# Feed-forward rows turned by VectorE and DMA, two weight loads issued by ScalarE, input rows read a group sooner

## The chip, the cores and the metric

The kernel runs on one core of a Trainium2 chip. The metric is the device time of one execution in microseconds; the time before is the median of three runs. The profile is of one further execution.

## The reference

x has the shape (4, 512, 512): four batches of 512 tokens of 512 features, f32. Four blocks follow one another, each added to the residual x:

```
x = x + attention_a(layernorm(x))   # 16 heads of 128, 4 key/value heads: half causal softmax with rotary,
                                    # half a gated linear recurrence over the tokens; then Wo
x = x + ffn(layernorm(x))           # ternary weights w1, w2 (1408x512) and w3 (512x1408)
x = x + attention_b(layernorm(x))   # 16 heads; weights are FP4 codes times a scale for each 32 rows
x = x + ffn(layernorm(x))

def ffn(x):
    x1, x2 = x @ quantize(w1).T, x @ quantize(w2).T
    return (sigmoid(x1) * x2) @ quantize(w3).T
```

The layernorm has no gain or bias: (x - mean) / sqrt(var + 1e-5).

## The kernel before

x stays in SBUF in 16 tiles of 128 tokens by 512 features (x0 to x15), four tiles (chunks) to a batch. Every product contracts over features, so normalised rows must be turned round: features on partitions. In the feed-forwards and in the second attention an f32 operand is kept as a rounded half hi and a remainder lo, both float32r, and each product is made twice, with hi and with lo.

**First attention** (`first_attention_gentle`). The steps are chunks: 4 batches by 4 key/value groups by 4 chunks of 128 tokens, so a group is four steps. `step(n)` issues the pieces of several chunks interleaved: A is the query projection (mm<-wq,xnT), B its softmax, rotation and a transfer through DRAM (queries, qdT), C transposes, D scores and softmax, own the recurrence's scores in a chunk (sc<-qdT,kdT), F the weighted values, G the output projection (mm<-wo,oT) with the add to x. TensorE's order in these steps is written by hand (`manual_schedule`); the other engines are ordered by the scheduler, except where `in_place` keeps an instruction where the program has it. Each group needs its Wq and its Wo (1 MB each, 16 loads of each). `load` reads the next batch's four x tiles at the first step of the group before, and `layernorm_steps` is advanced piece by piece by `next(ln)`: statistics (bn_stats, bn_aggr, POOL's power, three Newton steps), then for each chunk xn on VectorE, four transposes on TensorE into a tp bank, and a copy. All loads named here are on SyncE's queue. Beside this runs `quantise`, which makes the feed-forward's ternary weights and writes them to DRAM (`blocks`). `ahead(50, 0)` makes the first feed-forward's rows of batch 0 in the last steps, and the transposes for batch 1 follow where the scheduler puts them.

**Feed-forward** (`feed_forward`). The weights are loaded once for each feed-forward, in 22 loads (line 262). For each batch b: for each of 11 f, 16 products (sc<-xnhi,block and sc<-xnlo,block), sigmoid on ScalarE, hT on VectorE, hi on ScalarE, hlo on VectorE; then for each of 4 chunks c a product y of 22 matmuls (mm), the add to x and, in the second feed-forward, the store of the output. While batch b is computed, `halved` makes the rows of batch b + 1 by `layernorm_steps`: xn, four transposes (line 165), a split from PSUM into xnhi and xnlo (lines 120 and 121). All 512 tokens of a batch are the moving operand of its first products, so these need all four chunks. A caller's `next(steps)` per f from f = 2 on (two at f = 2) advances it.

During the first feed-forward the second attention prepares its weights (`prepare`): for each half weight a fetch (a load of the codes and four of the scales, SyncE, lines 284 and 287), two multiplications on POOL (line 292), two roundings on ScalarE (line 297), two comparisons on VectorE (line 303) and a write to DRAM (line 304). There are three such tiles.

xn has one buffer (`bufs=1`) in the pool `lnp`.

Of the kernel before, what the change touches and what calls it, by code (L numbers as in the profile page):

```python
# [9 lines left out]
F32 = mybir.dt.float32  # L10
# [9 lines left out]
P = 128  # L20
B, S, C = 4, 512, 512
NC = S // P
# [52 lines left out]
def hybrid_block(ctx: ExitStack, tc: tile.TileContext, a: dict, out: bass.AP):  # L75
# [42 lines left out]
    def split(hi, lo, src, engine=nc.vector):  # L118

        nc.scalar.copy(hi, src)  # L120
        engine.tensor_tensor(lo, src, hi, ALU.subtract)

    def layernorm_steps(b, sink, tag="tp", apart=False):

        mv = lnp.tile([P, NC, 2], F32, tag="mv", name="mv")
        rstd = lnp.tile([P, NC], F32, tag="rstd", name="rstd")

        def moments(c):  # L130
            st = lnp.tile([P, 6], F32, tag="st", name="st")
            nc.vector.bn_stats(st, xs[b * NC + c])  # L132
            nc.vector.bn_aggr(mv[:, c, :], st)

        def scales(at):

            var = lnp.tile([P, NC], F32, tag="var", name="var")[:, at]
            nc.vector.tensor_scalar(var, mv[:, at, 1], LN_EPS, None, ALU.add)
            r = rstd[:, at]
            nc.gpsimd.tensor_tensor(r, var, power[:, : r.shape[1]], ALU.pow)  # L140
            t = lnp.tile([P, NC], F32, tag="newton", name="newton")[:, at]
            nc.vector.tensor_tensor(t, r, r, ALU.mult)
            nc.vector.tensor_tensor(t, t, var, ALU.mult)
            nc.vector.tensor_scalar(t, t, -0.5, 1.5, ALU.mult, ALU.add)
            nc.vector.tensor_tensor(r, r, t, ALU.mult)

        if not apart:
            for c in range(NC):
                moments(c)
                if c == 1:  # L150
                    yield
            scales(slice(0, NC))
        for c in range(NC):
            if apart:
                moments(c)
                scales(slice(c, c + 1))
            else:
                yield
            xn = lnp.tile([P, C], F32, tag="xn", name="xn", bufs=1)
            nc.vector.tensor_scalar(xn, xs[b * NC + c], mv[:, c, 0:1], rstd[:, c : c + 1], ALU.subtract, ALU.mult)  # L160
            if not apart:
                yield
            tp = bank(tag, [P, NK, P])
            for k in range(NK):
                nc.tensor.transpose(tp[:, k, :], xn[:, k * P : (k + 1) * P], ident)  # L165
            sink(c, tp)
# [5 lines left out]
    def halved(pool, b):  # L172

        halves = [pool.tile([P, NK, S], F32R, tag=f"xn{n}", name=f"xn{n}") for n in ("hi", "lo")]
        return halves, layernorm_steps(b, lambda c, tp: split(*(h[:, :, c * P : (c + 1) * P] for h in halves), tp))

    def whole(pool, b):

# [31 lines left out]


    pieces = [[(k, f, n) for k in range(NK) for f, n in ((0, 6), (6, NF - 6))]] * 2 + [[(0, f, 1) for f in range(NF)]]
    part = per.tile([P, 3, NF], F32, tag="part", name="part")
    thr = per.tile([P, 3, 2], F32, tag="thr", name="thr")

    def quantise(pool, tag):


        def piece(n, k, f, m):
            w = pool.tile([P, 6 * P], F32, tag="w", name="w")[:, : m * P if n < 2 else C]  # L220
            if n < 2:
                in_place(nc.sync.dma_start(w, a[f"w{n + 1}T"][k * P : (k + 1) * P, f * P : (f + m) * P]))
            else:
                in_place(nc.sync.dma_start(w, a["w3T"][f * P : (f + 1) * P, :]))
            return w

        for n in range(3):
            for i, p in enumerate(pieces[n]):
                w = piece(n, *p)
                yield  # L230
                in_place(nc.scalar.activation(w, w, AF.Abs, accum_out=part[:, n, i : i + 1]))
                yield
            row = pool.tile([P, 1], F32, tag="row", name="row")
            nc.vector.tensor_reduce(row, part[:, n, : len(pieces[n])], AX.X, ALU.add)
            yield
            tot = bank(tag, [P, 1])
            nc.tensor.matmul(tot, lhsT=ones, rhs=row, start=True, stop=True)

            up, down = thr[:, n, 0:1], thr[:, n, 1:2]
            nc.vector.tensor_scalar(up, tot, 1.0 / (C * FF), QUANT_EPS, ALU.mult, ALU.add)  # L240
            nc.vector.tensor_scalar(down, up, -0.5, None, ALU.mult)
            nc.vector.tensor_scalar(up, up, 0.5, None, ALU.mult)
            yield
            for k, f, m in pieces[n]:
                w = piece(n, k, f, m)
                yield
                low = pool.tile([P, 6 * P], BF16, tag="low", name="low")[:, : w.shape[1]]
                in_place(nc.vector.tensor_scalar(low, w, down, None, ALU.is_lt))
                t = pool.tile([P, 6 * P], F32R, tag="tern", name="tern", bufs=1)[:, : w.shape[1]]
                in_place(nc.vector.scalar_tensor_tensor(t, w, up, low, ALU.is_gt, ALU.subtract))  # L250
                yield
                if n < 2:
                    in_place(nc.sync.dma_start(blocks[f : f + m, :, n, k * P : (k + 1) * P].rearrange("f p j -> p f j"), t.bitcast(F32).rearrange("p (f j) -> p f j", j=P)))
                else:
                    in_place(nc.sync.dma_start(blocks[f, :, n, :], t.bitcast(F32)))
# [53 lines left out]
    def first_attention_gentle(base, extra):  # L309
# [6 lines left out]
        with ExitStack() as st:  # L316
# [55 lines left out]
            class Group:  # L372
# [8 lines left out]

                def load_wq(self):
                    self.wq = one.tile([P, NK, HG * D], F32, tag="wq", name="wq")
                    nc.sync.dma_start(self.wq, a["Wq"][:, self.g * HG * D : (self.g + 1) * HG * D].rearrange("(k p) n -> p k n", p=P))

                def load_wo(self):
                    self.wo = late.tile([P, HG, C], F32, tag="wo", name="wo")
                    nc.sync.dma_start(self.wo, a["Wo"][self.g * HG * D : (self.g + 1) * HG * D, :].rearrange("(h p) n -> p h n", p=P))

                def project(self, c):  # L390
                    acc = bank("mm", [P, 2, D])
# [158 lines left out]
            def step(n):  # L550
                nonlocal ln
                m, p = divmod(n + 7, NC)
                at = lambda i: chunks.get(n + i) if n + i < last else None
                if (m + 1) % KV == 0 and (m + 1) // KV < B:
                    if p == 0:
                        load((m + 1) // KV)
                    if p == 1:
                        ln = normalise((m + 1) // KV)
                    if p > 1:
                        next(ln)  # L560
# [514 lines left out]
    def feed_forward(base, last, first):  # L1075

        with ExitStack() as st:
# [5 lines left out]
            ws = [block((soon, soon) if f < 2 else pools, f) for f in range(NF)]  # L1083
            xn = first
            for b in range(B):
                ready, steps = halved(base, b + 1) if b + 1 < B else (None, iter(()))
                hid = []
                for f, (w, _) in enumerate(ws):
                    xs12 = []
                    for n in range(2):  # L1090
                        x12 = bank("sc", [P, S])
                        project(x12, lambda i: w[:, n, i // 2 * P : (i // 2 + 1) * P], lambda i: xn[i % 2][:, i // 2, :], 2 * NK)
                        xs12.append(x12)
                    hT = two.tile([P, S], F32, tag="hT", name="hT")
                    nc.scalar.activation(hT, xs12[0], AF.Sigmoid)  # L1095
                    nc.vector.tensor_tensor(hT, hT, xs12[1], ALU.mult)
                    halves = [two.tile([P, S], F32R, tag=f"h{n}", name=f"h{n}", bufs=NF) for n in ("hi", "lo")]
                    split(*halves, hT)
                    hid.append(halves)
                    for _ in range((f > 1) + (f == 2)):  # L1100
                        next(steps, None)
                    yield b, f
                for c in range(NC):
                    y = bank("mm", [P, C])
                    project(y, lambda i: hid[i // 2][i % 2][:, c * P : (c + 1) * P], lambda i: ws[i // 2][1][:, 0, :], 2 * NF)
                    x = xs[b * NC + c]
# [6 lines left out]
    with banks(mm=2, sc=3, tp=2, pv=1), tc.tile_pool(name="base", bufs=2) as base:  # L1113
# [19 lines left out]
        for b, f in feed_forward(base, True, ffn_xn[1]):  # L1133
            if (b, f) == (B - 2, NF):

                fine = per.tile([P, KV * B + 4 * NG * NK], F32, tag="fine", name="fine")
                nc.vector.tensor_scalar(fine[:, : KV * B], steep, float(np.exp(GENTLE)), None, ALU.is_le)
                nc.vector.tensor_scalar(fine[:, KV * B :], inexact, 0.0, None, ALU.is_le)
                count = per.tile([P, 1], F32, tag="count", name="count")
                nc.vector.tensor_reduce(count, fine, AX.X, ALU.add)  # L1140
                redo = per.tile([P, 1], I32, tag="redo", name="redo")
                total = bank("mm", [P, 1])
                nc.tensor.matmul(total, lhsT=ones, rhs=count, start=True, stop=True)
# [48 lines left out]
```

## Time and profile before

| | |
|---|---|
| median of three runs | 2481.11 us (2479.9 to 2481.55) |
| the profiled execution | 2478.19 us |
| its span, first to last instruction | 2476.4 us |
| mean granted TensorE clock | 0.994 |
| TensorE busy | 2427.4 us, 98% |
| first attention | about 10 to 1045 us |
| first feed-forward | 1054.66 to about 1303 us |
| DMA issues: Wq, Wo | 16 each, 1024 KB, 5.7 and 5.9 us to landing |

PE is TensorE, PEld its weight loads, DVE VectorE, ACT ScalarE, POOL GpSimd, SP SyncE. `L165` is line 165 of the kernel. A group of instructions is named out<-in; a bracket at a line's end gives the idle time just before it and what ended it. The chain is what ended last, followed back from the end of the execution. Line numbers are those of the kernel before; in the changed kernel the hi copy of a feed-forward chunk is on line 213.

### The profile page before, as it was taken

To read this page: it belongs to the slowest core of one execution; us is meant where nothing else is said; L and a number is where in the kernel's file an instruction comes from. 1 tells how busy PE (TensorE), PEld (TensorE's weight loads), DVE (VectorE), ACT (ScalarE), POOL (GpSimd) and SP (SyncE) were. 2 spreads that over 40 slices of the span, in tenths; PEclk is the share of its full clock that TensorE was granted. 3 is DMA by queue.
4 is the path that set the end of the run, shared out by engine and by line. 5 is a ranking of instruction groups with operands and counts; after the bars stand their busy time and mean duration, and the time that the engine had idled before them with its cause. 6 is when DMAs were issued, how large, how long until landed. Compare 5 with 4: busy or idle time off the path is not lost.

```text
span 2476.4 us, 28996 instructions
## 1 busy us (share of the span) xinstructions
PE 2427.4 (98%) x8552; PEld 1544.3 (62%) x8552; DVE 1648.0 (67%) x3816; ACT 1209.7 (49%) x3066; POOL 387.7 (16%) x424
## 2 busy tenths in 40 slices
PE   7999999999999999899999999999999999999998
PEld 4545555555555555477886666666666666668887
DVE  6778777887878888456558666666766666664332
ACT  5756665666666665233326554444444444432222
POOL 1222222122222222022223333100000000000000
PEclk9999999999999999899999999999999999999999
DMA  4667765776656655475436777544343434333000
GB/s 146 190 176 208 209 190 176 206 208 181 187 174 196 196 176 165 127 230 149 128 107 187 200 185 221 146 115 116 94 131 93 125 93 132 89 92 132 18 18 19
DMA packets 240615, 367.10 MB, mean 148 GB/s; under 512 B 41664, under 2 KB 126912, under 8 KB 234304
## 3 DMA queue, kind: packets, MB, share of 16 engines
q1 hardware_dynamic: 231088, 338.58, 48.2%
q0 software_dynamic: 7680, 25.17, 3.5%
q8 instruction: 71, 1.16, 0.2%
q10 hardware_dynamic: 1680, 1.39, 0.2%
q14 instruction: 96, 0.79, 0.1%
HBM read 209.53 MB, written 88.34 MB: 120 GB/s over the span
## 4 chain that ended last, share of the span: by engine, by line
PE 89%; DVE 5%; issue 2%; ACT 1%; DMA 1%; SPq 1%; POOL 1%; DVEq 0%; POOLq 0%; ACTq 0%
PE mm L186 44%; PE sc L186 13%; PE sc L888 9%; PE pv L518 5%; PE sc L488 5%; PE pv L922 4%; PE tp L922 4%; PE sc L478 2%; PE pv L516 1%; PE tp L362 1%; PE tp L165 1%; SPq L915 1%; DVE st L132 0%; DVE xn L160 0%; DMA prT<-turned 0%
## 5 line engine op out<-in xcount | busy, mean ns | idle before, releaser
L893 ACT ACTIVATE pr<-sc,nm 128x512 f32<-128x512 f32 x256 | 175.8, 687 | 302.6 <-DVE nm L890 259.2
L186 PE MATMUL sc<-xnhi,block 128*128 128x512 f32 x704 | 276.9, 393 | 2.1 <-ACT hT L1095 2.1
L186 PE MATMUL sc<-xnlo,block 128*128 128x512 f32 x704 | 274.3, 390 | 0.0
L888 PE MATMUL sc<-kT,qT 128*128 128x512 f32 x512 | 262.0, 594 | 0.6 <-ACT kT L870 0.6
L186 PE MATMUL mm<-xnhi,w 128*128 128x512 f32 x512 | 254.1, 496 | 0.0
L186 PE MATMUL mm<-wq,xnT 128*128 128x512 f32 x512 | 232.2, 596 | 4.1 <-DVE x L191 2.0
L186 PE MATMUL mm<-wo,oT 128*128 128x512 f32 x512 | 232.8, 598 | 1.1 <-ACT oT L520 0.7
L890 DVE TENSOR_REDUCE nm<-sc 128x1 f32<-128x512 f32 x256 | 174.9, 683 | 74.3 <-PE sc L888 72.1
L186 PE MATMUL mm<-xnlo,w 128*128 128x512 f32 x512 | 205.9, 402 | 0.0
L910 DVE STREAM_TRANSPOSE turned<-pr 128x512 f32<-128x512 f32 x256 | 173.4, 696 | 37.0 <-ACT pr L900 34.0
L343 POOL TENSOR_TENSOR sw<-q_t,turn 128x256 f32<-128x256 f32 x128 | 98.8, 792 | 510.6 <-ACT q_t L451 441.2
L900 ACT ACTIVATE pr<-pr,den 128x512 f32<-128x512 f32 x192 | 138.2, 722 | 82.6 <-DVE den L898 82.6
L488 PE MATMUL sc<-krT,qrT 128*128 128x512 f32 (+3 forms) x512 | 170.4, 433 | 2.2 <-ACT pr L495 2.2
L497 ACT ACTIVATE pr<-pr,den 128x128 f32<-128x128 f32 (+3 forms) x256 | 141.7, 558 | 48.2 <-DVE den L496 46.3
L186 PEld LDWEIGHTS mm<-wq,xnT 128*128 128x128 f32 x512 | 96.4, 191 | 109.9 <-issue 99.1
L495 ACT ACTIVATE pr<-sc,nm 128x128 f32<-128x128 f32 (+3 forms) x256 | 132.6, 519 | 65.2 <-DVE nm L492 55.5
L498 DVE STREAM_TRANSPOSE turned<-pr 128x128 f32<-128x128 f32 (+3 forms) x256 | 128.6, 504 | 47.4 <-ACT pr L497 43.0
L186 PEld LDWEIGHTS mm<-wo,oT 128*128 128x128 f32 x512 | 96.8, 192 | 101.3 <-issue 96.0
L186 PEld LDWEIGHTS sc<-xnhi,block 128*128 128x128 f32 x704 | 132.2, 188 | 31.1 <-ACT hT L1095 2.9
L186 PEld LDWEIGHTS sc<-xnlo,block 128*128 128x128 f32 x704 | 132.2, 188 | 27.7 <-issue 0.7
L518 PE MATMUL pv<-prT,v_t 128*128 128x512 f32 x320 | 147.8, 592 | 0.0
L888 PEld LDWEIGHTS sc<-kT,qT 128*128 128x128 f32 x512 | 95.8, 189 | 81.6 <-issue 63.5
(151 smaller groups left out, 4801.5 us busy)
## 6 DMA issues: line engine op xcount, KB each, us to landing
prT<-turned SPq DMA_DIRECT2D x1024, 64.0 KB, 2.0
w<-exact SPq DMA_DIRECT2D x32, 1024.0 KB, 5.3
wq<-in_Wq SPq DMA_DIRECT2D x16, 1024.0 KB, 5.7
wo<-in_Wo SPq DMA_DIRECT2D x16, 1024.0 KB, 5.9
queries<-turned SPq DMA_DIRECT2D x64, 256.0 KB, 2.3
qdT<-queries SPq DMA_DIRECT2D x256, 64.0 KB, 3.0
passed<-turned SPq DMA_DIRECT2D x16, 1024.0 KB, 4.3
prT<-passed SPq DMA_DIRECT2D x64, 256.0 KB, 5.9
```

Source lines behind the costliest of these rows:

```text
L186: nc.tensor.matmul(acc, lhsT=lhs(k), rhs=rhs(k), start=k == 0, stop=k == n - 1)
L488: nc.tensor.matmul(sc.rearrange("p q (k j) -> p q k j", j=32), lhsT=self.qrT[:, h, :], rhs=self.k.krT.rearrange("p (k q j) -> p q k j", q= ...
L495: nc.scalar.activation(pr, flat, AF.Exp, bias=nm, scale=-1.0, accum_out=den)
L497: nc.scalar.mul(pr, pr, den)
L498: nc.vector.transpose(self.turned.rearrange("p (q h x) -> p q h x", q=4, h=HG)[:, :, h, :], pr.rearrange("p (q x) -> p q x", q=4))
L518: nc.tensor.matmul(acc.rearrange("p h (a t) -> p h a t", a=4), lhsT=self.k.v_t[:, j, :], rhs=self.wts[:, :, :, j, :], start=j == c == 0, s ...
L888: nc.tensor.matmul(sc, lhsT=qTs[u][:, i * P : (i + 1) * P], rhs=kTs[u], start=True, stop=True)
L890: nc.vector.tensor_reduce(nm, sc, AX.X, ALU.max, negate=True)
L893: nc.scalar.activation(pr, sc, AF.Exp, bias=nm, accum_out=den)
L900: nc.scalar.mul(pr, pr, den)
L910: nc.vector.transpose(turns[u][:, :, i, :], pr.rearrange("p (q k) -> p q k", q=4))
L922: nc.tensor.matmul(accs[u].rearrange("p (n t) -> p n t", t=32), lhsT=v_ts[m, j][:, h * D : (h + 1) * D], rhs=prTs[u].rearrange("p a i (k t ...
```

## The change

- For batches 1 to 3 of both feed-forwards the four TensorE transposes of a chunk (24 chunks, 96 transposes) give way to: a VectorE transpose of 32x32 blocks into the tile `turned` (one buffer), one DMA of 256 KB to DRAM (`rows`), four DMAs of 64 KB back into the tile `back`, a copy to hi by ScalarE and the subtraction for lo by VectorE, now from SBUF. `back` has the tag of xn, and so its one buffer. The DMAs are on SyncE's queue, in program order, as is the hi copy on ScalarE. `next(steps)` is called once for each f and once for each c.
- Wq and Wo of the first attention are issued by ScalarE, in program order.
- The x tiles of the next batch are read one group (four steps) earlier. The normalisation is still advanced at the steps it was advanced at; where its statistics stand on VectorE is the scheduler's choice.
- `part` moves to the pool of `quantise`; the final test of the two exactness tables is made in place, with two counts added, without the tile `fine`.

```diff
+    def halved_by_dma(pool, spare, b):
+        halves = [pool.tile([P, NK, S], F32R, tag=f"xn{n}", name=f"xn{n}") for n in ("hi", "lo")]
+        def steps():
+            moments, scales, rows = statistics(b)
+            for c in range(NC):
+                moments(c)
+            scales(slice(0, NC))
+            yield
+            for c in range(NC):
+                turned = spare.tile([P, 4, NK, 32], F32, tag="turned", name="turned", bufs=1)
+                nc.vector.transpose(turned.rearrange("p q k i -> p k q i"), rows(c).rearrange("p (k q j) -> p k q j", k=NK, q=4))
+                passed = dram.tile([P, C], F32, tag="rows", name="rows", bufs=3)
+                in_place(nc.sync.dma_start(passed, turned.rearrange("p q k i -> p (q k i)")))
+                yield
+                back = lnp.tile([P, C], F32, tag="xn", name="back", bufs=1)
+                for q in range(4):
+                    in_place(nc.sync.dma_start(back[32 * q : 32 * (q + 1)].rearrange("j (a x) -> j a x", a=4), passed.rearrange("(a j) (q x) -> q j a x", a=4, q=4)[q]))
+                yield
+                if c < 2:
+                    yield
+                hi, lo = (h[:, :, c * P : (c + 1) * P].rearrange("p k (a i) -> p k a i", a=4) for h in halves)
+                back = back.rearrange("p (a k i) -> p k a i", a=4, k=NK)
+                in_place(nc.scalar.copy(hi, back))
+                nc.vector.tensor_tensor(lo, back, hi, ALU.subtract)
+                yield
+        return halves, steps()
...
                 def load_wq(self):
-                    nc.sync.dma_start(self.wq, ...)
+                    in_place(nc.scalar.dma_start(self.wq, ...))
                 def load_wo(self):
-                    nc.sync.dma_start(self.wo, ...)
+                    in_place(nc.scalar.dma_start(self.wo, ...))
...
+                if p == 0 and (m + 2) % KV == 0 and (m + 2) // KV < B:
+                    load((m + 2) // KV)
                 if (m + 1) % KV == 0 and (m + 1) // KV < B:
-                    if p == 0:
-                        load((m + 1) // KV)
...
-                ready, steps = halved(base, b + 1) if b + 1 < B else (None, iter(()))
+                ready, steps = halved_by_dma(base, two, b + 1) if b + 1 < B else (None, iter(()))
...
-                    for _ in range((f > 1) + (f == 2)):
-                        next(steps, None)
+                    next(steps, None)
                     yield b, f
                 for c in range(NC):
+                    next(steps, None)
                     y = bank("mm", [P, C])
```

`statistics(b)` holds the statistics and xn (`rows(c)`) that were written in `layernorm_steps` before; `layernorm_steps` now calls it.

More of the change, by code (lines that the diff above doesn't have):

```diff
@@ L121, in split, with statistics @@
         engine.tensor_tensor(lo, src, hi, ALU.subtract)
-    def layernorm_steps(b, sink, tag="tp", apart=False):
+    def statistics(b):
         mv = lnp.tile([P, NC, 2], F32, tag="mv", name="mv")
@@ L145, in scales, with rows, layernorm_steps @@
             nc.vector.tensor_tensor(r, r, t, ALU.mult)
+        def rows(c):
+            xn = lnp.tile([P, C], F32, tag="xn", name="xn", bufs=1)
+            nc.vector.tensor_scalar(xn, xs[b * NC + c], mv[:, c, 0:1], rstd[:, c : c + 1], ALU.subtract, ALU.mult)
+            return xn
+        return moments, scales, rows
+    def layernorm_steps(b, sink, tag="tp", apart=False):
+        moments, scales, rows = statistics(b)
         if not apart:
@@ L158, in layernorm_steps @@
                 yield
-            xn = lnp.tile([P, C], F32, tag="xn", name="xn", bufs=1)
-            nc.vector.tensor_scalar(xn, xs[b * NC + c], mv[:, c, 0:1], rstd[:, c : c + 1], ALU.subtract, ALU.mult)
+            xn = rows(c)
             if not apart:
@@ L175, in halved @@
         return halves, layernorm_steps(b, lambda c, tp: split(*(h[:, :, c * P : (c + 1) * P] for h in halves), tp))
+    def halved_by_dma(pool, spare, b):
+        halves = [pool.tile([P, NK, S], F32R, tag=f"xn{n}", name=f"xn{n}") for n in ("hi", "lo")]
+        def steps():
+            moments, scales, rows = statistics(b)
+            for c in range(NC):
[20 more added lines that the diff above has]
+        return halves, steps()
     def whole(pool, b):
@@ L212, in hybrid_block @@
     pieces = [[(k, f, n) for k in range(NK) for f, n in ((0, 6), (6, NF - 6))]] * 2 + [[(0, f, 1) for f in range(NF)]]
-    part = per.tile([P, 3, NF], F32, tag="part", name="part")
     thr = per.tile([P, 3, 2], F32, tag="thr", name="thr")
     def quantise(pool, tag):
+        part = pool.tile([P, 3, NF], F32, tag="part", name="part", bufs=1)
         def piece(n, k, f, m):
@@ L383, in load_wq @@
                     self.wq = one.tile([P, NK, HG * D], F32, tag="wq", name="wq")
-                    nc.sync.dma_start(self.wq, a["Wq"][:, self.g * HG * D : (self.g + 1) * HG * D].rearrange("(k p) n -> p k n", p=P))
+                    in_place(nc.scalar.dma_start(self.wq, a["Wq"][:, self.g * HG * D : (self.g + 1) * HG * D].rearrange("(k p) n -> p k n", p=P)))
                 def load_wo(self):
                     self.wo = late.tile([P, HG, C], F32, tag="wo", name="wo")
-                    nc.sync.dma_start(self.wo, a["Wo"][self.g * HG * D : (self.g + 1) * HG * D, :].rearrange("(h p) n -> p h n", p=P))
+                    in_place(nc.scalar.dma_start(self.wo, a["Wo"][self.g * HG * D : (self.g + 1) * HG * D, :].rearrange("(h p) n -> p h n", p=P)))
                 def project(self, c):
@@ L1134, in hybrid_block @@
             if (b, f) == (B - 2, NF):
-                fine = per.tile([P, KV * B + 4 * NG * NK], F32, tag="fine", name="fine")
-                nc.vector.tensor_scalar(fine[:, : KV * B], steep, float(np.exp(GENTLE)), None, ALU.is_le)
-                nc.vector.tensor_scalar(fine[:, KV * B :], inexact, 0.0, None, ALU.is_le)
+                nc.vector.tensor_scalar(steep, steep, float(np.exp(GENTLE)), None, ALU.is_le)
+                nc.vector.tensor_scalar(inexact, inexact, 0.0, None, ALU.is_le)
+                counts = per.tile([P, 2], F32, tag="counts", name="counts")
+                for i, v in enumerate((steep, inexact)):
+                    nc.vector.tensor_reduce(counts[:, i : i + 1], v, AX.X, ALU.add)
                 count = per.tile([P, 1], F32, tag="count", name="count")
-                nc.vector.tensor_reduce(count, fine, AX.X, ALU.add)
+                nc.vector.tensor_reduce(count, counts, AX.X, ALU.add)
                 redo = per.tile([P, 1], I32, tag="redo", name="redo")
```

## The prediction

> **What bounds the kernel now.** I read the page first: busy times, then the shares of the chain.
>
> ```profile
> PE 2427.4 (98%) x8552; PEld 1544.3 (62%) x8552; DVE 1648.0 (67%) x3816; ACT 1209.7 (49%) x3066; POOL 387.7 (16%) x424
> ...
> PE 89%; DVE 5%; issue 2%; ACT 1%; DMA 1%; SPq 1%; POOL 1%; DVEq 0%; POOLq 0%; ACTq 0%
> ```
>
> TensorE is busy nearly throughout, so only what it executes, or waits for, counts. There are few such places, and the chain of waits shows them. In the first feed-forward (columns: start, us, engine and line):
>
> ```profile
> 1109.38 32.65 PE sc L186 x144
> 1142.04 0.44 PE tp L165 x4
> 1142.47 7.31 PE sc L186 x32
> 1149.79 0.44 PE tp L165 x4
> 1150.22 4.59 PE mm L186 x20
> 1154.82 0.01 issue
> 1154.82 0.68 DVE hT L1096
> 1155.50 0.46 DVE xn L160
> 1155.96 0.60 DVE xnlo L121
> 1156.56 0.61 DVE hlo L121
> ```
>
> Four transposes cost TensorE 0.44 us, and before the last hlo VectorE squeezes xn and xnlo in, so TensorE stands from 1154.82 to 1157.21. Then the end of the first attention, TensorE's and SyncE's timelines:
>
> ```profile
> 1005.49 1.13 PE L478 MATMUL sc<-qdT,kdT 128*128 128x512 f32 x2
> ...
> 1008.59 0.84 PE L165 MATMUL tp<-ident,xn 128*128 128x128 f32 x4 [1.87 <-DVE xn L160]
> ...
> 1011.62 1.09 PE L165 MATMUL tp<-ident,xn 128*128 128x128 f32 x4 [2.19 <-DVE xn L160]
> ...
> 1017.77 5.99 PE L186 MATMUL mm<-wo,oT 128*128 128x512 f32 x8
> ```
>
> ```profile
> 1007.23 0.40 SPq L388 DMA_DIRECT2D wo<-in_Wo  x1
> ```
>
> Transposes wait for xn, and the product behind them needs a Wo that is asked for only at 1007.23. Last, the boundaries between first-attention batches; the timeline of all engines shows the first:
>
> ```profile
> 129.76 0.69 DVE L132 BATCH_NORM_STATS2 st<-x 128x6 f32<-128x512 f32 x1 [1.59 <-DMA x<-in_hidden]
> ...
> 141.69 3.78 PE L186 MATMUL mm<-wkv,xnT 128*128 128x256 f32 x8 [4.79 <-DVE x L191]
> ```
>
> A group of four chunks normally takes 61.36 us (the 5.16 us piece of the chain recurs at 215.89, 277.25, 338.60). Over the three boundaries the intervals exceed this by 7.75, 4.52 and 3.55 us (beyond the 1.75 of the normalisation's own transposes, which stay): 15.8 in all, including late x, nine small VectorE instructions in a burst, and what follows them.
>
> The new transfers resemble ones already there (page, DMA issues; last column us to landing; and a group's row):
>
> ```profile
> queries<-turned SPq DMA_DIRECT2D x64, 256.0 KB, 2.3
> qdT<-queries SPq DMA_DIRECT2D x256, 64.0 KB, 3.0
> ```
>
> ```profile
> L459 DVE STREAM_TRANSPOSE turned<-qd 128x512 f32<-128x512 f32 x64 | 43.9, 686 | 0.0
> ```
>
> **Part by part.** The profiled execution took 2478.19 us, 1.79 more than its span; the median is 2481.11, so I add 2.9 at the end. 0.2% (5 us) is what a measurement here can tell from no change.
>
> 1. *Transposes in the feed-forward streams.* 18 of the 24 removed groups stand there: 18 x 0.44 = 7.9, and 0.8 of waiting for xn (groups of 2000 to 2250): **-8.7**.
>
> 2. *The y stall.* hT and hlo of the last f now stand together; this stall (2.39) and a like one at 1218.9 (0.3) go: **-2.7**.
>
> 3. *The tail of the first attention.* The other six groups stood at 996 to 1017. TensorE could go on at 1006.35, but for Wo. From ScalarE its load starts about 1006.0, behind a mul, not 1007.23; 7.4 us to landing, as in this row, is 1013.4 against 1017.77: **-4.4** (0 if Wo is later, -11.4 if it is no obstacle).
>
> 4. *x rows sooner.* One group (61 us) earlier, x is there, and the statistics spread into the group before. The 15.8 us hold TensorE's idle time at the boundaries (4.79, 2.02 and 1.7) and the slowed products behind it (3.78 and 5.40 instead of 3.43, 2.3 together): 10.8, which I take nearly whole, **-10** (0 if the burst only moves, -15.8 if all goes).
>
> 5. *Wq and Wo from ScalarE.* 32 issues x 0.396 us = 12.7 us on an engine that was busy 555 of 890 us here: **+1** (0 to +13). Behind each stand the copies and exponentials of the next chunk; they wait if the issue waits for its tile.
>
> 6. *The round trip.* Per chunk: xn 0.54, transpose 0.69, write issue 0.34 and landing 2.3, four reads issued in 1.75 and landing 3.0, hi 0.6, lo 0.69: about 10 us. xn and the read tile share one buffer, so the next chunk's xn waits for this lo; four chunks need 40 us at least. A block offers 60 (sc 40.3, y 20.0), so in principle it hides. What decides is where VectorE and SyncE, in the order of the built program, come to each step.
>
> *First feed-forward, block 0 to 1.* T is the end of sc (y ends at T+20.3). SyncE has 20 block loads ahead of the first write, and VectorE's lo of chunk 0 stands behind hT of the last f: nothing but chunk 0 is done before T. Turned 1 comes at T+2.75 (last hlo T+4.8, **+0.3**); its reads land T+10, lo 1 T+11.6. Turned 2 stands behind the x add of the third y, T+15.9; done T+16.6, written T+16.7. Then SyncE issues one fetch of the next weights (five issues, 2.7 us) ahead of chunk 2's reads, which land about T+24.4: lo 2 T+25.7. VectorE's next work before turned 3 is the comparison of those weights: fetch landing T+25.7 (8.4 us from first issue to POOL at 1092.41 to 1100.76), POOL 2.6, casts and comparisons: T+29.7. Turned 3 T+30.4; another fetch; chunk 3's reads land T+38.5, hi T+39.2. All of the next sc needs them: TensorE stands 19 us. After a pause TensorE is slower (5.99 for eight wo products at 1017.77, usually 3.60): 2 more. **+21**; +12 if fetch and comparison never get in the way (the buffer's chain alone gives hi 3 at T+32.6), +26 with slow landings.
>
> *Blocks 1 to 2 and 2 to 3.* Lo 2 stands behind the x add of the second y, turned 3 at T+12.9; fetch, then reads landing T+21, lo 3 behind another comparison, T+23: 2.8 us each, and some clock: **+6.5** for both (0 to +12).
>
> *Second feed-forward, 0 to 1.* Chunk 3's transpose stands behind the third x add (T+17.3), its write behind an output store; hi at T+24.7 against 20: **+5.5** with the clock (0 to +9). Later blocks finish by T+18: 0.
>
> VectorE's 24 transposes (16.5 us) cost nothing themselves: it is busy 86 of 140 us (2100 to 2240). They would cost up to 16.5 if it led. The count by in-place comparisons and part's move lie under y: nothing.
>
> The Trainium skill, "VectorE: DVE Perf Modes", rules for kernel authors, says to transpose 128x128 on TensorE where PSUM will do as a destination, which it does here; this speaks against the change. In this trace TensorE's way costs 0.44 us a chunk on the bound engine, the other 10 us of latency: by the row item 6 could still pay, were it hidden, and by the rule it should not have been moved, which would leave items 3 to 5 alone.
>
> The Trainium skill, "DMA: Bandwidth & Descriptors", rules for kernel authors, says that spreading issues over engines gives no bandwidth and saves issue time only. By it item 3 is at most the 1.2 us between the two issue times, not 4.4; the trace has the transposes going from in front of that load too, which the rule does not weigh, and no run here shows ScalarE's issue yet.
>
> Sum: -8.7 -2.7 -4.4 -10 +1 +0.3 +21 +6.5 +5.5 = **+8.5**: span 2484.9, profiled execution 2486.7, median 2489.6.
>
> **Rivals.**
>
> *A. The round trips hide (faster).* If the chain of block 0 to 1 ends by T+20.3, the 21 falls to 0: sum -12.5, median 2468.6. It decides at whether turned 3 is issued by about T+12: then write 2.6, reads 4.7 and hi end in time. For: 60 us offered, 40 needed. Against: one buffer, and turned 2 behind an add at T+15.9. If tail (-11.4) and boundaries (-15.8) give all, 2455.8.
>
> *B. ScalarE becomes late (slower).* A Wq or Wo issue that waits for its tile holds the exponentials behind it. For: TensorE's group is saturated (61.3 of 61.36 us), so every delay counts; against: ScalarE idles 38%. Full price 12.7 instead of 1: 2501.3.
>
> *C. Sooner x does not do what it is for.* The burst takes the time, not the wait: items 4 and 3 give nothing: sum +22.9, 2504.0. For: VectorE waited for x only 1.59 and 0.48 at the first boundary, 1.46 at the second; against: TensorE's 4.79 follows straight behind.
>
> **How the numbers follow.** Forecast 0.45, A 0.26, B 0.11, C 0.18. The forecast's own range is 2478 to 2500 (items 3, 4 and 6 half way to their bounds). For 8 in 10 I reach to the middle of A, 2466, and past C, 2508. Faster by over 0.2% (below 2476): nearly all of A and a little of the forecast, 0.28; within: 0.14 of the forecast; slower (over 2486): the rest, 0.58.
>
> **What would show it.** Right: in the chain, a pause of TensorE of 15 to 25 us at the end of the first block of the first feed-forward, released by hi (line 213); short ones at the next; no TensorE transposes there; the wo products after the first attention starting about 1013 less what the boundaries gave; intervals of 61 to 64 us at the boundaries. Wrong: no pause over 5 us at the block's end (A), ScalarE's issues as releasers and groups over 62 us (B), boundaries still over 66 (C).

## The result and the profile after

The changed kernel takes 2499.86 us (median of 6, 2498.32 to 2502.94) against 2479.07 us of the kernel before in the same comparison: ratio 1.0084, 95% interval 1.0074 to 1.0094. It is slower, by some 21 us; 2489.6 was forecast, in a range of 2466 to 2508. The profiled execution took 2498.32 us, with a span of 2496.5: 20.1 longer than before.

From the page, the busy times and one group of its list (columns of a group: busy us, mean ns of one, then the idle time before it and its releaser):

```profile
PE 2425.4 (97%) x8456; PEld 1539.5 (62%) x8456; DVE 1664.8 (67%) x3842; ACT 1211.2 (49%) x3066; POOL 390.0 (16%) x424
...
L228 PE MATMUL sc<-xnhi,block 128*128 128x512 f32 x704 | 282.7, 402 | 31.2 <-ACT xnhi L213 27.5
```

96 transposes fewer, and TensorE is busy only 2.0 us less, because products elsewhere ran slower; and there are 27.5 us in which the first products of a feed-forward block wait for hi (line 213), a wait that was not there. Where the time went, from the first product of each stage in the chain of waits:

| stage (us) | before | after | difference | forecast |
|---|---|---|---|---|
| first attention, to the first feed-forward's steady sc | 1054.66 | 1037.65 | -17.0 | -13.4 |
| first feed-forward | 247.01 | 280.14 | +33.1 | +22.5 |
| second attention | 920.42 | 921.65 | +1.2 | 0 |
| second feed-forward | 247.73 | 250.35 | +2.6 | -0.6 |

So the change holds a gain of 17 us and a loss of 37. The heart of the loss is the end of block 0 of the first feed-forward, in the chain of waits (start, us, what):

```profile
1074.00 14.97 PE mm L228 x66
...
1089.60 0.72 DVE turned L201
...
1090.73 0.43 SPq L327
...
1091.21 4.94 DMA raw<-in_wk_scales
...
1096.21 4.36 DMA exact<-raw
...
1101.97 0.69 DVE raw L346 x2
1102.66 0.46 DVE xn L148
...
1103.73 0.62 DVE turned L201
...
1104.77 5.17 DMA raw<-in_wv_codes
...
1109.96 3.21 DMA back<-rows
...
1113.33 0.63 ACT xnhi L213
```

Line by line this is the chain that the prediction wrote down with T = 1074.0: chunk 2 turned at T+15.6 (forecast T+15.9), the fetch ahead of its reads, the comparisons on VectorE ahead of chunk 3, chunk 3 turned at T+29.7 (T+29.7 to T+30.4), another fetch, hi at T+39.3 (T+39.2). TensorE ended y at 1094.0 and began sc again at 1115.39.

TensorE's waits over the whole first feed-forward:

```profile
PE sc L228 <- ACT xnhi L213: 24.4, 3, 20.1
PE sc L228 <- DVE xnlo L214: 4.3, 3, 2.2
```

28.7 us in three pauses. Behind each, sc runs at a lower clock, and so it does behind a pause of 3.1 us in the second feed-forward. The windows of four stretches (length, then busy time of each engine, then the granted clock, DMA share, GB/s) show the sc behind the four pauses; the sc of the kernel before have 1.00:

```profile
1115.40:1160.00 44.60, 44.60 (x185) 36.66 (x186) 25.99 (x41) 16.55 (x30) 9.02 (x6) 0.94 0.43 124
1182.50:1224.00 41.50, 41.43 (x176) 34.18 (x177) 23.83 (x39) 15.72 (x28) 8.45 (x6) 0.96 0.45 123
1248.30:1292.00 43.70, 43.67 (x186) 35.87 (x187) 19.97 (x34) 15.54 (x27) 8.58 (x9) 0.94 0.34 104
2305.80:2349.00 43.20, 43.20 (x177) 35.22 (x178) 19.22 (x29) 13.71 (x23) 0.00 (x0) 0.93 0.10 31
```

The first window holds 2.3 us of y as well: its 175 products of sc end at 1157.74, after 42.35 us. At full clock 176 take 39.89 (from 2369.01, behind no pause).

The end of the first attention, in TensorE's and ScalarE's timelines:

```profile
996.79 1.13 PE L521 MATMUL sc<-qdT,kdT 128*128 128x512 f32 x2
1001.40 5.35 PE L228 MATMUL mm<-wo,oT 128*128 128x512 f32 x8 [3.48 <-DMA wo<-in_Wo]
```

```profile
996.05 0.38 ACTq L431 DMA_DIRECT2D wo<-in_Wo  x1
```

4.61 us from own to the product with Wo instead of 12.28: a gain of 7.7. And the second boundary between batches, by the 5.16 us piece of the chain, once for each group:

```profile
336.32 5.16 PE mm L228 x16
...
397.68 5.16 PE mm L228 x16
...
461.46 5.16 PE mm L228 x16
```

The two groups take 61.36 and 63.78 us; before, the same two took 65.88 and 63.28 (338.60, 404.48, 467.76). At the last boundary's mark the changed kernel is 9.2 us ahead.

### The profile page after: what moved, and what is told of

Same layout as the page of the kernel before. It is cut to its first block, busy times and chain, and to the rows that moved or that the text cites. A ratio compares the mean times of both kernels' runs of the same rounds, so it can differ in the third digit from the quotient of the medians.

```text
span 2496.5 us, 29063 instructions
## 1 busy us (share of the span) xinstructions
PE 2425.4 (97%) x8456; PEld 1539.5 (62%) x8456; DVE 1664.8 (67%) x3842; ACT 1211.2 (49%) x3066; POOL 390.0 (16%) x424
## 4 chain that ended last, share of the span: by engine, by line
PE 87%; DVE 5%; DMA 4%; ACT 1%; issue 1%; SPq 1%; POOL 1%; ACTq 0%; DVEq 0%; POOLq 0%
PE mm L228 42%; PE sc L228 13%; PE sc L931 8%; PE pv L561 5%; PE sc L531 5%; PE tp L965 4%; PE pv L965 4%; PE sc L521 2%; PE pv L559 1%; PE tp L405 1%; SPq L958 1%; DMA back<-rows 1%; PE tp L175 1%; DMA x<-in_hidden 0%; DMA wo<-in_Wo 0%
## 5 line engine op out<-in xcount | busy, mean ns | idle before, releaser
L228 PE MATMUL sc<-xnhi,block 128*128 128x512 f32 x704 | 282.7, 402 | 31.2 <-ACT xnhi L213 27.5
L228 PE MATMUL sc<-xnlo,block 128*128 128x512 f32 x704 | 281.3, 400 | 4.3 <-DVE xnlo L214 4.3
```

Source lines behind the costliest of these rows:

```text
L228: nc.tensor.matmul(acc, lhsT=lhs(k), rhs=rhs(k), start=k == 0, stop=k == n - 1)
```

## The experiments

The theory to be tested: the parts add up; the feed-forwards' rows carry the whole loss, through a chain that VectorE's order, SyncE's queue and one buffer make long; Wq and Wo give the end of the first attention; the sooner x rows give the boundaries. Each has a rival. All ratios are against the kernel before on the same chip.

**1. Only the parts in the first attention** (feed-forward rows by TensorE as before).

```diff
-                ready, steps = halved_by_dma(base, two, b + 1) if b + 1 < B else (None, iter(()))
+                ready, steps = halved(base, b + 1) if b + 1 < B else (None, iter(()))
```

> The changed kernel with the feed-forward rows of all batches again by TensorE's transposes and the old schedule of steps; Wq and Wo by ScalarE and the sooner x rows stay. Theory (the parts add up; all of the loss is the feed-forwards' round trip): the three boundaries give 9.2 us as in the changed kernel, the end of the first attention 3 to 4 of its 7.8 (the transposes still stand there); 2479 becomes 2466 (2464 to 2470), with no pause over 1 us between feed-forward blocks. Rival (ScalarE's issues cost something that the changed kernel's profile hides): 2475 or more.

Measured: 2473.71 us (12 runs, 2468.73 to 2482.18), ratio 0.9976 (0.9966 to 0.9985). A gain of some 6, less than either part alone gives below, outside the theory's 2464 to 2470 and short of the rival's 2475; no pauses between blocks. In its profile the last boundary's mark comes 7.2 us sooner, not 9.2, and the end of the first attention gives 1.6, not 3 to 4: behind its wait for the last Wo the eight products take 5.40 us (3.70 in 3). The medians of 1, 3 and 4 lie within 3 us, and the runs of this one are 13 apart, so their order is not settled.

**2. Only the feed-forward rows.**

```diff
-                    in_place(nc.scalar.dma_start(self.wq, ...))
+                    nc.sync.dma_start(self.wq, ...)
...
-                if p == 0 and (m + 2) % KV == 0 and (m + 2) // KV < B:
-                    load((m + 2) // KV)
+                    if p == 0:
+                        load((m + 1) // KV)
```

(Wo likewise.)

> The kernel before with only the feed-forward rows turned by VectorE and DMA; Wq and Wo by SyncE and x rows as before. Theory: it carries the whole loss. TensorE idle 20.7, 4.2, 3.9 and 3.1 us at the ends of four blocks, the slower clock after each, less the transposes: about +37 against the first feed-forward's start; the end of the first attention without transposes but with the late Wo gives 3 back: 2479 becomes 2512 (2505 to 2516). Rival (the loss needs ScalarE's queue or the sooner start as well): under 2500.

Measured: 2512.81 us, ratio 1.0133 (1.0118 to 1.0147): 33 us slower, as expected. From the first steady sc to the end of the span it takes 1458.3 us, the changed kernel 1458.9, the kernel before 1421.7. So the loss is in these rows, whole: 30.8 us in the first feed-forward. They also bring the one gain that was expected of them: sc starts at 1050.39 instead of 1054.66, since no transposes stand in the end of the first attention. What stands there then is Wo:

```profile
1013.64 5.88 PE L228 MATMUL mm<-wo,oT 128*128 128x512 f32 x8 [7.89 <-DMA wo<-in_Wo]
```

**3. Only Wq and Wo by ScalarE; 4. only the x rows sooner.** (The two hunks of the change, each put on the kernel before.)

> The kernel before with only the loads of Wq and Wo issued by ScalarE. Theory: SyncE is freed, and the last Wo lands sooner: -3 to -5, 2475, all at the end of the first attention; the boundaries between batches keep their 15.8 us. Rival: the boundaries' loss was SyncE's queue (x rows issued late behind other waits), so that the boundaries shrink here too and the whole is -8 or more.

> The kernel before with only the x rows read one group sooner. Theory: this part alone gives the boundaries' 9.2: 2479 becomes 2470 (2468 to 2473), the intervals at the three boundaries 63.1 to 64 us. Rival (the waits move to another load, since SyncE still issues Wq and Wo): less than 5 us gained.

Measured: 3 takes 2470.83 us, ratio 0.9971 (0.9960 to 0.9982); 4 takes 2471.99, ratio 0.9967 (0.9954 to 0.9980). 4 is as the theory had it. 3 is as its rival had it: the boundaries shrink here too. From the 5.16 us piece after the first boundary to the last one of the first attention (215.89 to 902.74 before, two boundaries in between) it is 686.85 us before, 682.02 in 3, 683.61 in 4, 680.64 in 1, 679.93 in the changed kernel. So either part alone takes most of the boundaries' loss, and both together little more than one.

In 3, x is not there sooner (SyncE issues it at 126.50, before at 123.03). What changed is VectorE's order: the rotation (lines 341, 344) now stands ahead of the first statistics, and the add to x behind one of them (138.53), where in the kernel before the four statistics at 126 to 131 stood ahead of both and the add came at 140.95. From VectorE's timeline of 3:

```profile
133.49 1.21 DVE L344 TENSOR_TENSOR qr<-qr,sw 128x512 f32<-128x512 f32 x1
135.81 0.67 DVE L132 BATCH_NORM_STATS2 st<-x 128x6 f32<-128x512 f32 x1
138.53 0.64 DVE L191 TENSOR_TENSOR x<-x,mm 128x512 f32<-128x512 f32 x1
```

TensorE's 4.79 us of idle time at 141.69 is gone in both. The rest of 3's gain is the end of the first attention: sc starts at 1042.12, 12.5 sooner, of which 8.1 stand already at the last boundary's mark (894.61 instead of 902.74).

**5. VectorE's feed-forward work held in program order.**

```diff
-                    nc.vector.tensor_tensor(hT, hT, xs12[1], ALU.mult)
+                    in_place(nc.vector.tensor_tensor(hT, hT, xs12[1], ALU.mult))
```

(The same for hlo, xn, the 32x32 transpose, lo and the add to x.)

> The changed kernel with VectorE's work of the feed-forward (hT, hlo, xn, the 32x32 transpose, lo, the add to x) held in the order of the program, so that lo of chunk 0 stands after hT of the fifth f, not after the last, and chunk 3 is turned during the first y. Buffers, transfers and SyncE's order stay. Theory (the pause at the end of a block is VectorE's order: the chain starts too late): the pauses at the ends of the blocks, 20.7, 4.2 and 3.9 us in the first feed-forward, fall to under 3 us each; in the first block about 7 us of TensorE waiting appear instead in the middle of sc, where VectorE waits for the reads of chunk 0 behind the block loads; in all 2500 becomes 2476 (2470 to 2484). Rival (one shared buffer and the fetches on SyncE's queue bound the chain wherever it starts): the pauses only move, over 25 us of waiting stay, 2490 or more.

Measured: 2491.63 us, ratio 1.0061 (1.0045 to 1.0078): 8 better than the changed kernel by the medians, not 24. TensorE's waits in the first feed-forward of this kernel:

```profile
PE mm L230 <- DVE x L1153: 14.4, 4, 8.8
PE sc L230 <- DVE hT L1141: 3.5, 1, 3.5
PE sc L230 <- DVE xnlo L216: 2.5, 3, 1.1
```

The pauses at the block ends are nearly gone, and y waits instead, for adds to x that stand on VectorE behind a lo whose reads have not landed: 20.9 us instead of 28.7. VectorE's order made a part of the loss; most of it moved, as the rival had it, though less than its 25 us of waiting remain.

This kernel also tests the clock. In its second feed-forward no pause stands right ahead of the sc of batch 1, and there the 176 products of the 2305.80 window above take:

```profile
2300.87 39.89 PE sc L230 x176
```

The clock is 1.00 at the same DMA share of 0.10. So it is the pause that makes this sc slow, and not the transfers beside it.

**6. The pause filled with products that nobody uses.**

```diff
+                if b == 0 and not last:
+                    idle = bank("mm", [P, C])
+                    for _ in range(80):
+                        in_place(nc.tensor.matmul(idle, lhsT=ws[0][0][:, 0, :P], rhs=xn[0][:, 0, :], start=True, stop=True))
```

> The changed kernel with 80 further products of 512 columns on TensorE (18.3 us, their result is not used) between y of batch 0 and sc of batch 1 of the first feed-forward, that is inside the 21.4 us pause. Theory (a pause costs the clock of the products behind it too): the granted clock of the following sc stays at 1.00 instead of 0.94 and this sc takes 41 us instead of 44.6; 2500 becomes 2497. Rival (the slower sc has another cause, such as transfers or VectorE's lag): sc stays at 44 us or more, the time the same within 1 us.

Measured in that stretch: 175 products of sc take 41.58 us instead of 42.35. The 44.6 of the expectation is the window that holds 2.3 us of y, so 0.8 us went and not 3. The window of this sc:

```profile
1119.00:1160.60 41.60, 41.55 (x176) 34.25 (x177) 23.50 (x39) 16.32 (x29) 8.10 (x6) 0.96 0.43 126
```

The clock is at 0.96, not 1.00: 3.3 us of waiting remain behind the 80 products, and this short pause still costs 1.9 of the 2.7 us of clock. So filling most of the pause hardly helped, and this run alone does not settle between theory and rival. The whole execution shows no gain: 2505.72 (2497.98 to 2508.88), ratio 1.0111 (1.0095 to 1.0126), 6 more than the changed kernel. In its profile, which is of the shortest of the four executions (2497.98), the first feed-forward starts 4.6 us later, with TensorE waiting for Wo 1.9 us at 952 (0.3 in the changed kernel) and 3.8 at 1005 (3.5 at 1001 there) and slower products behind both; nothing of the edit lies there. What the edit does to the median stays open.

**7. The weight fetches by GpSimd.**

```diff
-            count, does = prepare(lambda: room((0, 1, "r")[next(turn) % 3]), range(NG // 2), nc.sync)
+            count, does = prepare(lambda: room((0, 1, "r")[next(turn) % 3]), range(NG // 2), nc.gpsimd)
```

> The changed kernel with the second attention's weight fetches and writes during the first feed-forward issued by GpSimd instead of SyncE. VectorE's order is nearly unchanged: the comparisons still stand ahead of the third and fourth transposes. Theory: of the first pause (20.7 us) only what SyncE's issues in front of the reads of chunks 2 and 3 cost goes, 5 to 9 us; the later pauses shrink by 2 us each: 2500 becomes 2490 (2486 to 2495). Rival (SyncE's queue is the cause): the pauses of the first feed-forward go almost whole, 2476 or less.

Measured: 2497.86 us, ratio 1.0071 (1.0056 to 1.0087): 2 better than the changed kernel by the medians, which the intervals do not tell from nothing, where 10 were expected. Its profile is of an execution of 2505.59 us, the longest of the four, and is read for its order only: the first pause is 15.7 us instead of 20.1, and the block loads on SyncE's queue now take 22.47 us to issue instead of 13.16, so that sc itself waits 2.7 us for a block. Taking the fetches off the queue does not take them off the path; the rival (2476 or less) falls.

**10. The preparation kept out of the first block.**

```diff
-            next(attention)
+            for _ in range((0, 2, 1, 1)[b]):
+                next(attention)
```

> The changed kernel with the second attention's weight preparation left out of the first block of the first feed-forward and done at twice the pace in its second block, so that in the first block no fetch stands on SyncE's queue, no comparison on VectorE and no weights on the DMA engines beside the four round trips. In the order built, chunk 1 is turned after hT of the ninth f, chunk 3 after the x add of the third y. Theory (the first pause is the preparation's work inside the chain): it falls from 20.7 to about 4 us; the pause of the second block grows by 2 to 5; in all 2500 becomes 2487 (2483 to 2491). Rival (the chain of one shared buffer takes its time without the preparation too): the first pause stays at 12 or more.

Measured: 2504.54 us, ratio 1.0100 (1.0084 to 1.0115), 5 slower than the changed kernel by the medians. The first pause does fall to 3.2 us, as the theory said; the second and third grow to 15.8 and 12.0 from 4.2 and 3.9. Waits over the first feed-forward:

```profile
PE sc L228 <- ACT xnhi L213: 29.3, 3, 15.0
PE sc L228 <- DVE xnlo L214: 1.7, 2, 0.9
```

31.0 us in all, against 28.7. In the first block the pause goes with the preparation, and one reason shows in the landing times. The reads of a chunk, first in the changed kernel beside fetches (1074 to 1116), then here ahead of the first fetch (1069 to 1097; it is issued at 1095.09):

```profile
back<-rows SPq DMA_DIRECT2D x12, 64.0 KB, 4.3
```

```profile
back<-rows SPq DMA_DIRECT2D x12, 64.0 KB, 2.0
```

From VectorE's transpose to the start of lo it is 6.8 us alone (1079.83 to 1086.64) and 10.9 beside fetches (1089.60 to 1100.46). Four trips of 7 fit into a block of 60 us nearly as VectorE orders them. Four of 11 would make 44 and fit too, so the place of each trip decides. In the second and third block VectorE turns chunk 3 only behind the last add to x (T+24.2 and T+21.7), in the changed kernel behind the second (T+12.5 and T+12.4). In the third block the preparation has the same pace in both kernels, so that pause is VectorE's order, and not the amount of preparation. Of the 7.9 us by which the spans of the two profiles differ, another 4.7 stand in the second attention; their cause stays open.

**9. The changed kernel with x rows as before.** (The x hunk taken back.)

> The changed kernel with the x rows read where they were before; Wq and Wo by ScalarE and the feed-forward rows by VectorE and DMA stay. Theory (Wq and Wo alone already free the boundaries, the sooner x adds nothing to them): the first feed-forward starts at 1038 to 1040 us, the whole is 2499 to 2502. Rival (in the changed kernel the sooner x rows carry the boundaries, as the prediction had it): 2506 or more.

Measured: 2500.68 us, ratio 1.0091 (1.0076 to 1.0105): the same as with the sooner rows. The stages are not so equal: the first feed-forward starts at 1043.01 (outside the 1038 to 1040 of the theory), 5.4 later than in the changed kernel. The first sc (34.77 us instead of 36.35) and the second (41.74 behind the pause instead of 42.35) give 2.2 of that back at a better clock; the later stages give back most of the rest. The stretch of two boundaries is 682.14 us, as in 3: the sooner x rows are worth 2 us there once ScalarE issues the weights.

**8 and 11. What pays, together.** From the runs above: Wq and Wo by ScalarE, x rows as before, TensorE's transposes held in the feed-forward so that none stands in the end of the first attention, the steps begun at the first f. 8 keeps VectorE and DMA for batches 2 and 3 of the second feed-forward, where the changed kernel shows no pause; 11 has none of it.

```diff
+                dma = last and b + 1 in (2, 3)          # 11: dma = False
+                make = (lambda pool, b: halved_by_dma(pool, two, b)) if dma else (lambda pool, b: halved(pool, b, True))
...
+                if pin:
+                    in_place(op)                        # each of the four transposes of a chunk
...
+                    for _ in range(1 if dma else f < NF - 1):
+                        next(steps, None)
```

> What seems to pay: Wq and Wo by ScalarE; x rows as before; TensorE's transposes in the first feed-forward and for batch 1 of the second, but held at their place in the feed-forward, so that none stands in the end of the first attention; VectorE and DMA for batches 2 and 3 of the second feed-forward only; the steps begin at the first f. Theory: boundaries -8, end of the first attention -8, six transposes back in the stream +2.6, eight out of it -3.9, the y stall -2.7: 2479.5 becomes 2460 (2456 to 2465). Rival (with the transposes out of the way the last Wo ends the gap as late as in Wq and Wo alone): 2466 or more.

> The best mix without any rows by VectorE and DMA: Wq and Wo by ScalarE, x rows as before, all feed-forward transposes on TensorE and held at their place in the feed-forward. Theory: eight groups of four transposes return to the second feed-forward, +3.6 against the best mix: 2466 (2463 to 2468). Rival (the VectorE way costs as much there as it saves): 2463 or less.

Measured: 8 takes 2462.63 us, ratio 0.9939 (0.9925 to 0.9953), the fastest of all, 16 below the kernel before and within its theory. 11 takes 2469.06, ratio 0.9958 (0.9945 to 0.9972), 1 above the range of its theory. In 8, TensorE waits 2.5 us in the whole first feed-forward. The eight chunks that VectorE and DMA turn are worth 6 by the medians, whose intervals overlap, and 2.8 by the spans of the two profiles (2464.4 and 2467.2). The second feed-forward itself, from its first sc to the end of its last y, takes 245.8 in 8 and 248.7 in 11: 2.9 less; 3.6 was expected. So without the preparation beside it the round trip does hide.

One part of 8 came out as its rival had it: in the profiled execution (2466.16) the end of the first attention gives 3.1 behind the last boundary's mark, not 8. TensorE waits 3.5 us for the last Wo, and its eight products take 6.74. The faster executions of 8 have no profile.

A buffer of its own for the reads was not tried, so how much of the loss the one shared buffer makes stays open.

## Why the prediction was right, and where its sum was off

**Direction and cause held.** The forecast was slower, by a pause of TensorE at the end of the first block; experiment 2 puts the whole loss on the rows, and the chain of that pause agrees with the one written down to within 1 us at each step. The sum was +8.5 and the spans say +20.1.

**Item 1, -8.7, and item 2, -2.7** have no experiment of their own. The transposes are gone from the streams of the changed kernel, and the wait of 1154.82 with them. The busy time of TensorE fell by 2.0 only, since the slower clock put back most of what the transposes had taken.

**Item 3, -4.4, was low: -7.7.** Wo was asked for at 996.05, 0.7 ahead of own, where 0.5 behind it had been taken; and the load landed some 5.3 us later, not 7.4. The term was within its bound of -11.4. Experiments 2 and 3 part it: without the transposes but with the late Wo sc starts 4.3 sooner (0.9 of it already at the last boundary's mark), with the sooner Wo but with the transposes 4.4 come behind that mark.

**Item 4, -10, had the right size, but not one owner.** The mark at the last boundary came 9.2 us sooner, and the mechanism is there: in the changed kernel and in 4 the first boundary's statistics stand at 77 to 84 us, a group before. But the sooner x rows are not the only way to it. Wq and Wo alone give 8.1 at the mark (3): with the same late x it was enough that the statistics no longer stood ahead of the rotation and the add. Without the sooner rows the changed kernel has its mark at 897.77, 5.0 sooner than before (9). The forecast gave the whole to the x rows and nothing to Wq and Wo, and that was wrong; once these are moved, the rows are worth 2.2 us over the two boundaries between the marks.

**Item 5, +1.** ScalarE's issues cost nothing that the runs show; rival B, that it becomes late, is refuted by 3, which is faster with nothing else changed. What the change did add is a new wait: in every kernel with Wo by ScalarE whose profile was read there (the changed one, 1, 3 and 5 to 11) TensorE waits 0.3 to 1.9 us for the next to last Wo at about 950, in those with Wo by SyncE (before, 2, 4) not at all; in 6 and 8 the eight products behind it take 5.40 us instead of 3.70. That was not foreseen, and by its size it can make part of the spread between runs.

**The rule on issuing engines.** The Trainium skill, "DMA: Bandwidth & Descriptors", rules for kernel authors, says that spreading issues over engines saves issue time only. Experiment 3 does nothing else, and gains 8.7 us by the medians. The rule may hold for the transfers, whose landing hardly changed (5.7 and 5.9 us before, 5.5 and 6.1 after), but it does not bound the gain: an issue that leaves a queue lets everything behind it, and the order of other engines with it, move.

**Item 6, block 0 to 1, +21.** The pause was 20.7 us of waiting, 19 forecast; the clock behind it cost 2.7 (42.35 us for products that take 39.7 at full clock), 2 forecast. **Blocks 1 to 2 and 2 to 3, +6.5, were mis-sized:** 4.2 and 3.9 us of waiting instead of 2.8 each, and 1.7 and 2.6 of clock instead of some 0.9 in all: 12.4. **The second feed-forward, +5.5:** 3.1 of waiting instead of 4.7, and 3.0 of clock (43.2 us at 0.93) instead of 0.8: 6.1. The stage is still 3.2 above its forecast, because of waits that the sum did not have: 1.0 us for a block load and 0.7 for hT in its first sc, 0.7 for an add to x in its third y, none of them in the kernel before.

**So the largest error of the sum is the clock.** The lost share of the granted clock times the length of the stretch, over the four sc behind pauses and the first sc (36.4 us at 0.95, 1.8), makes 11.8 us; the forecast had allowed 3.7. This term was mis-sized, the mechanism was named. That the pause makes it is shown for the second feed-forward, where the same sc takes 43.28 us behind the pause and 39.89 in 5 without it; filling the first pause to 3.3 us took only 0.8 of the 2.7 away (6). The forecast priced the clock by eight products (5.99 instead of 3.60); what it costs is a stretch of some 5 us at nearly half speed: behind the first pause the products step at 0.427 us from 1115.98 to 1120.68 and at 0.228 from 1121.0 on.

**Rival A** (the round trips hide) fails in the changed kernel and is true in its second feed-forward for batches 2 and 3 (but for 0.7 us of waiting for an add), which 8 uses. **Rival C** (the boundaries keep their loss) is refuted by the 61.36 and 63.78 us and the 9.2 at the last mark.

**The rule on transposes.** The Trainium skill, "VectorE: DVE Perf Modes", rules for kernel authors, would leave 128x128 transposes on TensorE where PSUM will do. In the first feed-forward the runs agree with it (30.8 us lost there in 2); for the eight chunks of 8 the traces decide the other way, by 2.9 us in that stage.

## What to carry to other kernels

A round trip through DRAM is hidden or not by the place of each of its instructions in the order of each engine, not by the time that the stage offers: write down that order, with what is queued in front of every step, and sum the chain against the end of the cover. Where a chain shares the DMA engines and an in-order engine with another stream of work, moving the work about moved most of the pause (5, 10); look for a stage where that stream is absent. And price a pause of the bound engine at more than itself: here the four of 3.1 to 20.7 us cost 2 to 3 us of slower clock each besides.

## What the runs showed of the hardware

- The four pauses of 3.1 to 20.7 us cost nearly the same in clock, with no relation to their length: the granted clock was 0.93 to 0.96 over the 41 to 45 us behind them, 1.7 to 3.0 us each.
- Behind shorter waits it came in some executions and not in others. After 1.9 us of waiting for Wo eight products took 3.70 us in 1 and 11 and 5.40 in 6 and 8; after 3.4 us they took 3.70 in 10 (clock 1.00) and 5.38 in 11 (0.69).
- Transfers of 64 KB landed in 2.0 us with little else under way (DMA engines 19% busy, 1069 to 1097 in experiment 10), and in 4.3 beside fetches (62% busy, 1074 to 1116 in the changed kernel), by the medians.
- After an idle time of 2.09 us the first sc took 34.77 us in some executions (the kernel before, 2, 6, 9) and 36.3 in others (the changed kernel, 1, 3, 4, 10), with the same wait in front of it.
